# A decoder layer on one core: the context's load, the keys' tile and the routing's constants between two attentions

## The chip, the cores and the metric

The kernel runs on one core of one Trainium2 chip. The core has five engines with a queue each: TensorE (PE, matrix products; its weight loads are listed as PEld), VectorE (DVE), ScalarE (ACT), GpSimd (POOL) and SyncE (SP, which here only issues transfers). The metric is the device time of one execution in microseconds (us). An engine works through its own instructions in their order and waits where an operand is not ready; the framework puts semaphores between the engines.

## The reference

The layer takes x (16 batches of 128 tokens, 256 wide) and a context (16 batches of 128 positions, 64 wide), all float32. Cut to what matters:

```python
# 1. gated delta rule: 16 key heads, 32 value heads of 128, a scan over 128 tokens
mixed = silu(conv4(x @ w_qkv)); q, k, v = split(mixed); z = x @ w_z
S = S * exp(g);  S = S + k (v - k S) beta;  o = q S
x = layernorm(x + (rms_norm(o * silu(z)) * norm_w) @ w_out)
# 2. cross attention: 32 query heads of 8, 8 key heads; keys = values = context
x = layernorm(x + softmax(q k^T / sqrt(8)) v)
# 3. seven routed experts, each token to its best two, and one shared expert
u = x @ Wup + bup; g = silu(u @ Wgate + bgate) * u; y = g @ Wdown + bdown
x = layernorm(x + sum_e p_e * y_e + shared(x))
```

## The kernel before

The tokens of a batch lie on the 128 partitions; x stays in SBUF as `acc` (128 x 16 x 256) for the whole program.

**First attention.** Sixty-four units (four groups of four batches, times 16 key heads) go through a pipeline written as one loop over steps `s` (from L577 on). A step works on several units at once, each in another state: projections and convolution, decay products, blockwise solution of the triangular system, output. On SP the loop issues for later units the loads of weights (`wkq` L311, `wv` L324, `wz` L329, `wo` L334) and of decays (`dec` L316). GpSimd inverts the small triangular blocks (L275, L277) and takes powers for norms (L459, L106). In this loop GpSimd runs in the order in which the program is written (`manual_schedule`); the other engines' orders are planned by the framework ahead of time from its own estimates, so that instructions can be placed earlier than where they are written.

The output weights are scaled once: `scale_wo` (L160 to L171) is written in steps 5 to 12, eight rounds, each for two heads. A round loads two parts of `w_out` into the tile `wor` (one buffer, so that a round's loads wait for the stores of the round before), scales it on ScalarE (L168) and stores both parts to DRAM (`wo_d`, L170). Units load them from there.

The attention ends with a layer norm of the last four batches: statistics, a power on GpSimd (L106), and one pass per batch on VectorE (L111).

**Between the attentions.** The first attention's pools are closed and new ones opened over the same memory; in the trace nothing is written there before the attention's last accumulation (L471) has ended. Then come, as written: the context's load into `ctx_sb` (L678 to L680), the loads of the experts' weights on SP (L687 to L696), the tile `vext` with all 16 batches' keys, padded to 32 columns a head (cleared, ones in column 8, keys copied in, L707 to L711), the two query tiles `xq` cleared (L713 to L715), and the constants that only the routing needs: `zero` and its 12 transfers that clear the routed rows `xg` (L723 to L729), `tri`, `allones`, `ival`, `full` (L730 to L740), `probs`, `wrev` and `count` (L855 to L1020).

**Second attention.** Per batch, class `Cross`. `keys` spreads the context four times (`crep`, L754, GpSimd), turns it and the batch's part of `vext` on TensorE (L758, L759), copies the result on ScalarE (`kt`, L762) and masks it on GpSimd (`km`, L765). `queries` turns x1 on TensorE (L773), copies it on ScalarE (`x1T`, L775) and copies it into one of two padded tiles on GpSimd (`xq`, L777). Then, in 64 steps of two heads, `largest` computes scores and their maxima (L787, L791), `shifted` writes the maxima into `xq` and turns it (L795, L801), `exps` computes scores again and their exponentials (L810, L815), `weighted` multiplies these by `vext` (L824), and `end` and `back` bring the result into `acc` (L834 to L850). The loop that writes this runs from n = -7 on, with `largest` seven steps ahead of `exps`. In it `keys` and `queries` of batch 0 are written ahead of the loop, of batch 1 at n = -5, of batch 2 at n = -1, of batch 3 at n = 3. GpSimd's written order starts at n = 0. What is written before that, GpSimd's part of batches 0 to 2, is placed by the planner.

Routing and experts follow: scatter of rows to the experts by indirect transfers on GpSimd's queue (L1007), experts on 44 row tiles, gather, shared expert, last layer norm.

Of the kernel before, what the change touches and what calls it, by code (L numbers as in the profile page):

```python
# [8 lines left out]
F32 = mybir.dt.float32  # L9
# [3 lines left out]
ALU = mybir.AluOpType  # L13
# [3 lines left out]
P = 128  # L17
B, S, H = 16, 128, 256
HK, HV = 16, 32
G = 4  # L20
# [3 lines left out]
NE = 8  # L24
# [8 lines left out]
TILES = (2 * HB * P - (NE - 1)) // P + NE - 1  # L33
# [8 lines left out]
def decoder_kernel(  # L42
# [7 lines left out]
    nc = tc.nc  # L50
    vec, act, pool, pe = nc.vector, nc.scalar, nc.gpsimd, nc.tensor

    const = ctx.enter_context(tc.tile_pool(name="const", bufs=1))
    big = ctx.enter_context(tc.tile_pool(name="big", bufs=1))


    ident = const.tile([P, P], F32, name="ident")
# [22 lines left out]


    acc = big.tile([P, B, H], F32, name="acc")
    xv = x.rearrange("b s h -> s b h")

    def load_x(g):
        nc.sync.dma_start(out=acc[:, g * G : (g + 1) * G, :], in_=xv[:, g * G : (g + 1) * G, :])
# [28 lines left out]
    with ExitStack() as st:  # L115
# [28 lines left out]
        sb = st.enter_context(tc.tile_pool(name="sb", bufs=2))  # L144
# [14 lines left out]

        def scale_wo(i):  # L160

            wor = sb.tile([P, 2, G, P], F32, tag="wor", bufs=1, name=f"wor{i}")
            wor = wor.rearrange("p k b t -> p k (b t)").rearrange("p k (r n) -> p k r n", r=2)
            for k in range(2):
                hk = 2 * i + k
                nc.sync.dma_start(out=wor[:, k], in_=w_out[hk * 256 : (hk + 1) * 256, :]
                                  .rearrange("(r p) n -> p r n", p=P))
            act.activation(wor, wor, AF.Copy, scale=normw)  # L168
            for k in range(2):
                nc.scalar.dma_start(out=wo_d[2 * i + k], in_=wor[:, k])  # L170
# [376 lines left out]
        with tc.manual_schedule(engines={mybir.EngineType.Pool}):  # L547
            for s in range(NU + DELAY + 3):
                a, v, m = at(s), at(s - DELAY + 1), at(s - DELAY)
                p, q, o = at(s - DELAY - 1), at(s - DELAY - 2), at(s - DELAY - 3)  # L550
# [4 lines left out]
                k, ph = s // U - 1, s % U  # L555
# [32 lines left out]
                    at(s + 1).load_dec()  # L588
                if 0 < s < NG:
                    load_x(s)  # L590
                if s == U:
                    piece(0)
                    gates([1, 2, 3])
# [73 lines left out]
    late = ctx.enter_context(tc.tile_pool(name="late", bufs=1))  # L667
# [7 lines left out]
    def bank2(shape, name):  # L675
        return ps2.tile(shape, F32, tag="ps", name=name)

    ctx_sb = cx1.tile([P, B, 8, 8], F32, name="ctx_sb")  # L678
    nc.sync.dma_start(out=ctx_sb.rearrange("p b k d -> p b (k d)"),
                      in_=ctx_512.rearrange("b s d -> s b d"))  # L680

    wup = late.tile([P, NE, 2, H], F32, name="wup")
    wgt = late.tile([P, NE, 2, H], F32, name="wgt")
# [15 lines left out]
    for i, src in enumerate((bsu, bsg)):  # L699
# [4 lines left out]

    vext = cx1.tile([P, B, 8, 32], F32, name="vext")  # L707
    pool.memset(vext, 0.0)
    pool.memset(vext[:, :, :, 8:9], 1.0)
    pool.tensor_copy(vext[:, :, :, 0:8].rearrange("p b k d -> p (b k) d"),  # L710
                     ctx_sb.rearrange("p b k d -> p (b k) d"))  # L711

    xqs = [cx1.tile([P, 4, 8, 32], F32, name=f"xq{i}") for i in range(2)]  # L713
    for t in xqs:
# [5 lines left out]
    dram2 = ctx.enter_context(tc.tile_pool(name="dram2", bufs=1, space=DRAM))  # L720
    xg = [dram2.tile([TILES * P, H], F32, name=f"xg{h}") for h in range(NH)]
    yg = [dram2.tile([TILES * P, H], F32, name=f"yg{h}") for h in range(NH)]
    zero = late.tile([P, 4, H], F32, name="zero")  # L723
    pool.memset(zero, 0.0)
    for t in xg:
        for i in range(0, TILES, 4):
            n = min(4, TILES - i)
            nc.sync.dma_start(out=t[i * P : (i + n) * P, :].rearrange("(t p) d -> p t d", p=P),
                              in_=zero[:, :n, :])  # L729
    tri = late.tile([P, P], F32, name="tri")  # L730
    pool.memset(tri, 1.0)
    pool.affine_select(out=tri, in_=tri, pattern=[[1, P]], compare_op=ALU.is_ge, fill=0.0,
                       base=-1, channel_multiplier=-1)
    allones = late.tile([P, P], F32, name="allones")
    pool.memset(allones, 1.0)
    ival = late.tile([P, TILES], F32, name="ival")
    for i in range(TILES):
        pool.memset(ival[:, i : i + 1], float(i))
    full = late.tile([P, NE], F32, name="full")
    vec.tensor_scalar(full, ival[:, :NE], float(P), None, ALU.mult)  # L740

    class Cross:


# [4 lines left out]

        def keys(self):  # L750
            bi = self.bi

            crep = cx.tile([P, 8, 4, 8], F32, tag="crep", name=f"crep{bi}")
            pool.tensor_copy(crep, bc(ctx_sb[:, bi, :, None, :], [P, 8, 4, 8]))  # L754
            crf = crep.rearrange("p k g d -> p (k g d)")
            pkt = bank2([P, 2, 2, P], f"pkt{bi}")
            for c in range(2):
                pe.transpose(pkt[:, 0, c, :], crf[:, c * P : (c + 1) * P], ident)  # L758
                pe.transpose(pkt[:, 1, c, :],  # L759
                             vext[:, bi, 4 * c : 4 * c + 4, :].rearrange("p k d -> p (k d)"), ident)  # L760
            self.kt = cx.tile([P, 2, 2, P], F32, tag="kt", bufs=3, name=f"kt{bi}")
            act.copy(self.kt, pkt)  # L762
            self.km = cx.tile([P, 2, 4, P], F32, tag="km", name=f"km{bi}")
            for c in range(2):
                pool.tensor_tensor(self.km[:, c], bc(self.kt[:, 0, c, None, :], [P, 4, P]),  # L765
                                   bc(g_mask[:, :, None], [P, 4, P]), ALU.mult)
# [51 lines left out]
        def weighted(self, kvs):  # L818

            for kv in kvs:  # L820
                if kv % 4 == 0:
                    self.pav = pav_pool.tile([P, 4, P], F32, tag="pav", name=f"pav{self.bi}_{kv}")
                r = (kv % 4) * 32
                pe.matmul(self.pav[r : r + 32].rearrange("p g t -> p (g t)"),  # L824
                          lhsT=vext[:, self.bi, kv, :],
                          rhs=self.ex.pop(kv).rearrange("p g t -> p (g t)"), start=True, stop=True)
                if kv % 4 == 3:
                    self.end(kv // 4)
# [23 lines left out]

    NR = NE - 1
    probs = late.tile([P, B, NE], F32, name="probs")
    pool.memset(probs, 1.0)  # L855
    pT = late.tile([NE, B, P], F32, name="pT")
    wrev = late.tile([P, NR], F32, name="wrev")
    for e in range(NR):
        pool.memset(wrev[:, e : e + 1], float(NR - e))

    class Route:

# [153 lines left out]
        return [late.tile(shape, dt, name=f"{name}{h}") for h in range(NH)]  # L1016

    count = per_half([P, NR], "count")
    for t in count:
        pool.memset(t, 0.0)  # L1020
    ranks = per_half([P, HB, NR], "ranks")
    chosen = per_half([P, 2, HB, NR], "chosen")
    rows = per_half([P, 2, HB], "rows", U32)
# [10 lines left out]
    LEAD = 7  # L1034
    crosses = [Cross(bi) for bi in range(B)]
    steps = [(bi, (2 * h, 2 * h + 1)) for bi in range(B) for h in range(4)]
    crosses[0].keys()
    crosses[0].queries()
    later = {}
    for n in range(-LEAD, len(steps) + 3):  # L1040
        if n == 0:
            in_order = ctx.enter_context(ExitStack())
            in_order.enter_context(tc.manual_schedule(engines={mybir.EngineType.Pool}))
        if 0 <= n + 1 < len(steps) and (n + 1) % 4 == 0:
            crosses[(n + 1) // 4].shifted()
# [185 lines left out]
    r = routes[NG - 1]  # L1231
# [67 lines left out]
```

## Time and profile before

| what | us |
|---|---|
| time, median of three runs | 2191.08 (2190.01 to 2192.49) |
| the profiled execution's own time | 2189.38 |
| its span, first to last instruction | 2186.8 |
| TensorE busy | 2040.9 (93%) |
| VectorE, ScalarE, GpSimd busy | 1740.3, 1316.1, 1077.0 |
| start, 0 to 130: TensorE busy | 57.95 of 130.00 |
| first attention's body, 130 to 1743.5: TensorE busy | 1578.11 of 1613.50 |
| between, 1743.5 to 1758.8: TensorE busy | 0.05 of 15.30 |
| second attention, 1758.8 to 1959.4: TensorE busy | 193.68 of 200.60 |
| rest, experts and end, 1959.4 to 2186.8: TensorE busy | 211.13 of 227.40 |

A profile shows one execution. In its timeline a line gives start, length, engine, line of the program, operation, output and inputs with shapes, and in brackets how long the engine was idle before and which engine's instruction ended that. Stretches give, for each engine, busy time and number of instructions; then TensorE's granted clock (1.00 is full), the share of the transfer engines and GB/s. An idle stretch is put down to the signal that came last, by inference; lines of waits give total, number and longest.

### The profile page before, as it was taken

The page shows a single profiled execution, that of the slowest core. Times are in us where ns is not written, and L with a number is a line of the kernel's source. Part 1 is how long each engine was busy: PE and PEld are TensorE (multiplying, and loading weights), DVE is VectorE, ACT ScalarE, POOL GpSimd, SP SyncE. Part 2 cuts the span into 40 slices and gives each one's busy share as a digit, 9 for nine tenths or more (in the row PEclk, how much of TensorE's full clock was granted, in tenths as well). Part 3 has the DMA queues.
Part 4 walks back from the last instruction along what each step waited for, and adds up shares of the span by engine and source line. Part 5 has one row for each costly group of instructions (what it writes and reads, how often), then busy time and mean ns, then how long its engine had stood idle before and what let it go on. Part 6 is the DMA issues. An engine that isn't in the chain of part 4 may idle for free.

```text
span 2186.8 us, 40366 instructions
## 1 busy us (share of the span) xinstructions
PE 2040.9 (93%) x14688; PEld 1242.5 (57%) x14688; DVE 1740.3 (80%) x3223; ACT 1316.1 (60%) x2696; POOL 1077.0 (49%) x1639
## 2 busy tenths in 40 slices
PE   4559999999999999999999999999989879989997
PEld 2324556566565666665666656656656534448873
DVE  4657889898999989898999989898856667866545
ACT  4536666667666667666676666676656445554431
POOL 0136473838465564739384655648372143352222
PEclk7779999999999999999999999999999979999998
DMA  6412222222222222222221222222011070013321
GB/s 195 137 48 54 59 59 71 61 65 66 59 64 68 64 64 64 62 69 59 68 64 59 71 61 68 64 59 59 30 40 30 23 262 1 1 56 105 110 80 58
DMA packets 140660, 150.72 MB, mean 69 GB/s; under 512 B 14184, under 2 KB 111472, under 8 KB 140464
## 3 DMA queue, kind: packets, MB, share of 16 engines
q1 hardware_dynamic: 133456, 135.37, 21.9%
q0 software_dynamic: 3072, 8.39, 1.2%
q10 hardware_dynamic: 3936, 4.38, 0.6%
q8 instruction: 118, 1.93, 0.4%
q14 instruction: 78, 0.64, 0.1%
HBM read 125.82 MB, written 22.28 MB: 68 GB/s over the span
## 4 chain that ended last, share of the span: by engine, by line
PE 72%; POOL 10%; DVE 8%; ACT 4%; issue 3%; DMA 3%; SPq 0%; ACTq 0%; POOLq 0%; DVEq 0%
PE pp L467 9%; PE pjv L339 8%; PE pjz L339 8%; PE pjkq L339 8%; PE pt L520 6%; PE po L452 5%; PE pu L505 5%; PE pk L399 4%; PE psc L787 3%; POOL Tp L277 2%; POOL tmp L275 2%; PE pv L439 2%; PE psq L482 2%; PE prg L1123 2%; PE pru L1123 2%
## 5 line engine op out<-in xcount | busy, mean ns | idle before, releaser
L524 ACT COPY u<-pt 32x512 f32<-32x512 f32 x512 | 294.4, 575 | 57.1 <-PE pt L520 48.4
L339 PE MATMUL pjkq<-xT,wkq 128*128 128x512 f32 x512 | 246.0, 621 | 55.9 <-issue 47.3
L509 DVE TENSOR_TENSOR u<-u,pu 32x512 f32<-32x512 f32 x384 | 263.6, 687 | 37.9 <-PE pu L505 27.0
L365 POOL TENSOR_TENSOR yv<-yv,y2v 128x508 f32<-128x508 f32 x128 | 161.8, 1264 | 255.2 <-DVE yv L356 231.8
L467 PE MATMUL pp<-wo,og 128*128 128x256 f32 x1024 | 272.1, 395 | 0.0
L277 POOL TENSOR_TENSOR Tp<-Tp,tmp 128x240 f32<-128x240 f32 (+14 forms) x465 | 253.6, 545 | 36.4
L275 POOL TENSOR_TENSOR tmp<-Tp 128x240 f32<-128x240 f32 (+14 forms) x465 | 239.6, 515 | 62.0 <-DVE Tp L277 33.8
L356 DVE SCALAR_TENSOR_TENSOR ykq<-pjkq,cw,ykq 128x504 f32<-128x504 f32 (+2 forms) x384 | 266.2, 725 | 2.8 <-ACT ykq L349 2.3
L356 DVE SCALAR_TENSOR_TENSOR yv<-pjv,cw,yv 128x504 f32<-128x504 f32 (+1 forms) x256 | 188.9, 738 | 98.7 <-ACT y2v L353 91.6
L339 PE MATMUL pjv<-xT,wv 128*128 128x512 f32 x512 | 250.2, 612 | 16.8 <-issue 7.0
L471 DVE SCALAR_TENSOR_TENSOR acc<-pp,rstd,acc 128x256 f32<-128x256 f32 x512 | 231.5, 477 | 42.9 <-POOL rstd L459 37.1
L459 POOL TENSOR_TENSOR rstd<-var,m_half 128x8 f32<-128x8 f32 x64 | 105.4, 1648 | 320.7 <-DVE ss L493 272.3
L339 PE MATMUL pjz<-xT,wz 128*128 128x512 f32 x512 | 243.7, 598 | 5.9 <-issue 5.9
L366 ACT ACTIVATE vT<-yv 128x512 f32<-128x512 f32 x128 | 80.7, 630 | 252.2 <-POOL yv L365 252.2
L467 PEld LDWEIGHTS pp<-wo,og 128*128 128x128 f32 x1024 | 183.5, 190 | 78.5 <-issue 57.2
L339 PEld LDWEIGHTS pjkq<-xT,wkq 128*128 128x128 f32 x512 | 93.1, 194 | 184.1 <-issue 173.9
L402 DVE TENSOR_TENSOR lp<-pk,e 128x512 f32<-128x512 f32 x256 | 159.3, 682 | 39.7 <-PE pk L399 38.6
L520 PE MATMUL pt<-u,Tt 32*32 32x128 f32 x4096 | 176.2, 272 | 1.6 <-ACT u L442 1.0
L520 PEld LDWEIGHTS pt<-u,Tt 32*32 32x32 f32 x4096 | 116.4, 104 | 105.5 <-issue 35.1
L384 DVE TENSOR_TENSOR_SCAN e<-dec,ident 128x512 f32<-128x512 f32 x128 | 158.4, 1278 | 8.2 <-DMA dec<-dec_d 6.5
L452 PE MATMUL po<-lp,u 128*128 128x128 f32 x1024 | 152.2, 285 | 0.0
L442 ACT ACTIVATE u<-pv,nk 128x128 f32<-128x128 f32 x512 | 147.3, 374 | 6.5 <-PE pv L439 5.8
(226 smaller groups left out, 3619.6 us busy)
## 6 DMA issues: line engine op xcount, KB each, us to landing
dec<-dec_d SPq DMA_DIRECT2D x64, 512.0 KB, 5.2
wkq<-in_L_attn_w_qkv_dram SPq DMA_DIRECT2D x128, 128.0 KB, 5.1
wv<-in_L_attn_w_qkv_dram SPq DMA_DIRECT2D x64, 256.0 KB, 2.6
wz<-in_L_attn_w_z_dram SPq DMA_DIRECT2D x64, 256.0 KB, 2.6
wo<-wo_d SPq DMA_DIRECT2D x64, 256.0 KB, 2.7
rx<-xg SPq DMA_DIRECT2D x44, 128.0 KB, 2.1
yg<-ry SPq DMA_DIRECT2D x44, 128.0 KB, 1.7
xg<-zero SPq DMA_DIRECT2D x10, 512.0 KB, 7.8
```

The costliest lines, as they stand in the source:

```text
L275: eng.tensor_tensor(tv, bc(T[:, j + 1 :, j : j + 1], [P, n, j]), bc(T[:, j : j + 1, 0:j], [P, n, j]), ALU.mult)
L277: return eng.tensor_tensor(T[:, j + 1 :, 0:j], T[:, j + 1 :, 0:j], tv, ALU.add)
L339: pe.matmul(pj.rearrange("p b t -> p (b t)"), lhsT=ws[kc], rhs=xTs[self.g][:, kc, :], start=(kc == 0), stop=(kc == 1))
L356: inst = vec.scalar_tensor_tensor(out=y[:, :, d:], in0=pj[:, :, : P - d], scalar=c[:, k : k + 1], in1=y[:, :, d:], op0=ALU.mult, op1=ALU.add)
L365: pool.tensor_tensor(y[:, :, 1:], y[:, :, 1:], y2[:, :, 1:], ALU.add)
L402: self.made = vec.tensor_tensor(self.lp[:, r, hf * 2 : hf * 2 + 2], pk, bc(self.e[r][:, hf * 2 : hf * 2 + 2, None, :], [P, 2, 2, P]), ALU. ...
L452: pe.matmul(po[:, b, :], lhsT=self.u_[r][:, b, :], rhs=self.lp[:, r, b, 1, :], start=True, stop=True)
L467: pe.matmul(pp[:, r, :], lhsT=self.og[:, r, b, :], rhs=self.wo[:, r, :], start=True, stop=True)
L471: vec.scalar_tensor_tensor(out=a, in0=pp[:, r, :], scalar=self.rstd[:, r, b : b + 1], in1=a, op0=ALU.mult, op1=ALU.add)
L509: vec.tensor_tensor(u.u_[r][blk], u.u_[r][blk], pu[blk], ALU.subtract)
L520: pe.matmul(pt[blk, b, :], lhsT=groups[u.n // U].Tt[blk, 8 * u.u + G * r + b, :], rhs=u.u_[r][blk, b, :], start=True, stop=True)
L524: act.copy(u.u_[r][blk], pt[blk])
```

## The change

Four things change. (1) `ctx_sb` is made at the top, in the pool that lives through the program; the eight rounds of `scale_wo` use it as their tile `wor`, and the context is loaded into it in step 48 of the first attention's loop. (2) `vext` becomes four tiles of one batch each; all four are cleared and given their ones before the second attention, and `keys` copies its batch's keys into one of them in turn. (3) The routing's constants are written at n = 1 of the second attention's loop, behind `keys` and `queries` of batch 2. (4) GpSimd's written order starts ahead of `keys` of batch 0.

```diff
     acc = big.tile([P, B, H], F32, name="acc")
+    ctx_sb = big.tile([P, B, 8, 8], F32, name="ctx_sb")
...
         def scale_wo(i):
-            wor = sb.tile([P, 2, G, P], F32, tag="wor", bufs=1, name=f"wor{i}")
-            wor = wor.rearrange("p k b t -> p k (b t)").rearrange("p k (r n) -> p k r n", r=2)
+            wor = ctx_sb.rearrange("p b k d -> p (b k d)").rearrange("p (k r n) -> p k r n", k=2, r=2)
...
                 if 0 < s < NG:
                     load_x(s)
+                if s == 3 * HK:
+                    nc.sync.dma_start(out=ctx_sb.rearrange("p b k d -> p b (k d)"),
+                                      in_=ctx_512.rearrange("b s d -> s b d"))
...
-    ctx_sb = cx1.tile([P, B, 8, 8], F32, name="ctx_sb")
-    nc.sync.dma_start(out=ctx_sb.rearrange("p b k d -> p b (k d)"),
-                      in_=ctx_512.rearrange("b s d -> s b d"))
...
-    vext = cx1.tile([P, B, 8, 32], F32, name="vext")
-    pool.memset(vext, 0.0)
-    pool.memset(vext[:, :, :, 8:9], 1.0)
-    pool.tensor_copy(vext[:, :, :, 0:8].rearrange("p b k d -> p (b k) d"),
-                     ctx_sb.rearrange("p b k d -> p (b k) d"))
+    vexts = [cx1.tile([P, 8, 32], F32, name=f"vext{i}") for i in range(4)]
+    for t in vexts:
+        pool.memset(t, 0.0)
+        pool.memset(t[:, :, 8:9], 1.0)
...
         def keys(self):
             bi = self.bi
+            self.vext = vexts[bi % 4]
+            pool.tensor_copy(self.vext[:, :, 0:8], ctx_sb[:, bi])
...
+    in_order = ctx.enter_context(ExitStack())
+    in_order.enter_context(tc.manual_schedule(engines={mybir.EngineType.Pool}))
     crosses[0].keys()
     crosses[0].queries()
     later = {}
     for n in range(-LEAD, len(steps) + 3):
-        if n == 0:
-            in_order = ctx.enter_context(ExitStack())
-            in_order.enter_context(tc.manual_schedule(engines={mybir.EngineType.Pool}))
+        if n == 1:
+            pool.memset(probs, 1.0)
+            for e in range(NR):
+                pool.memset(wrev[:, e : e + 1], float(NR - e))
+            for t in count:
+                pool.memset(t, 0.0)
+            zero = late.tile([P, 4, H], F32, name="zero")
+            pool.memset(zero, 0.0)
+            for t in xg:
+                for i in range(0, TILES, 4):
+                    k = min(4, TILES - i)
+                    nc.sync.dma_start(out=t[i * P : (i + k) * P, :].rearrange("(t p) d -> p t d", p=P),
+                                      in_=zero[:, :k, :])
+            tri = late.tile([P, P], F32, name="tri")
+            pool.memset(tri, 1.0)
+            pool.affine_select(out=tri, in_=tri, pattern=[[1, P]], compare_op=ALU.is_ge, fill=0.0,
+                               base=-1, channel_multiplier=-1)
+            allones = late.tile([P, P], F32, name="allones")
+            pool.memset(allones, 1.0)
+            ival = late.tile([P, TILES], F32, name="ival")
+            for i in range(TILES):
+                pool.memset(ival[:, i : i + 1], float(i))
+            full = late.tile([P, NE], F32, name="full")
+            vec.tensor_scalar(full, ival[:, :NE], float(P), None, ALU.mult)
```

The same constants' lines are removed from where they stood, and the products with the keys' tile (L824) and its transposes (L759) read the batch's own tile.

More of the change, by code (lines that the diff above doesn't have):

```diff
@@ L722, in decoder_kernel @@
     yg = [dram2.tile([TILES * P, H], F32, name=f"yg{h}") for h in range(NH)]
[L723 to L740, printed above, removed]
     class Cross:
@@ L759, in keys @@
                 pe.transpose(pkt[:, 1, c, :],
-                             vext[:, bi, 4 * c : 4 * c + 4, :].rearrange("p k d -> p (k d)"), ident)
+                             self.vext[:, 4 * c : 4 * c + 4, :].rearrange("p k d -> p (k d)"), ident)
             self.kt = cx.tile([P, 2, 2, P], F32, tag="kt", bufs=3, name=f"kt{bi}")
@@ L824, in weighted @@
                 pe.matmul(self.pav[r : r + 32].rearrange("p g t -> p (g t)"),
-                          lhsT=vext[:, self.bi, kv, :],
+                          lhsT=self.vext[:, kv, :],
                           rhs=self.ex.pop(kv).rearrange("p g t -> p (g t)"), start=True, stop=True)
@@ L854, in decoder_kernel @@
     probs = late.tile([P, B, NE], F32, name="probs")
-    pool.memset(probs, 1.0)
     pT = late.tile([NE, B, P], F32, name="pT")
     wrev = late.tile([P, NR], F32, name="wrev")
-    for e in range(NR):
-        pool.memset(wrev[:, e : e + 1], float(NR - e))
     class Route:
@@ L1018, in decoder_kernel @@
     count = per_half([P, NR], "count")
-    for t in count:
-        pool.memset(t, 0.0)
     ranks = per_half([P, HB, NR], "ranks")
```

## The prediction

> **What bounds the kernel now.** I read the page's 40 slices first. Each is 54.7 us. The first line is TensorE's busy tenths, the second its granted clock:
>
> ```profile
> PE   4559999999999999999999999999989879989997
> PEclk7779999999999999999999999999999979999998
> ```
>
> From the fourth slice on TensorE is 8 or 9 tenths busy at nearly full clock, apart from slice 33 (1749 to 1804 us), where both digits are 7, and the last. So a change beside TensorE pays only at the start and at that dip. The dip lies between the two attentions. The waits of 1743 to 1790 us name it (total, times, longest):
>
> ```profile
> PE pkt L758 <- POOL crep L754: 15.3, 1, 15.3
> ```
>
> TensorE's last matmul of the first attention ends at 1743.55 and its next is at 1758.80: 15.25 us for a copy by GpSimd. GpSimd's timeline shows what stood before that copy (start, length):
>
> ```profile
> 1742.49 1.64 POOL L459 TENSOR_TENSOR rstd<-var,m_half 128x8 f32<-128x8 f32 x1 [7.25 <-DVE var L490]
> 1747.67 3.51 POOL L708 MEMSET vext<- 128x4096 f32 x1 [3.54 <-DVE acc L471]
> 1751.28 1.01 POOL L106 TENSOR_TENSOR rsa<-rsa,m_half 128x4 f32<-128x4 f32 x1
> 1752.24 0.95 POOL L715 MEMSET xq<- 128x1024 f32 x1
> 1753.12 0.31 POOL L709 MEMSET vext<- 128x128 f32 x1
> 1753.30 0.99 POOL L715 MEMSET xq<- 128x1024 f32 x1
> 1754.24 1.08 POOL L710 COPY vext<-ctx_sb 128x1024 f32<-128x1024 f32 x1
> 1755.27 1.09 POOL L724 MEMSET zero<- 128x1024 f32 x1
> ...
> 1758.35 0.40 POOL L754 COPY crep<-ctx_sb 128x256 f32<-128x256 f32 x1
> ```
>
> The reader is to see no idle time from 1747.67 on: GpSimd is the bound, not the context's transfer, which was issued at 1747.48 and landed 4.9 us later, at 1752.4, when GpSimd still had 5.9 us to do. (The chain of waits puts weights' transfers here. ScalarE's first copy of keys, which it hangs on them, reads only TensorE's transposes, over 0.03 us before.) VectorE runs beside, twice held:
>
> ```profile
> 1749.16 2.04 DVE L105 TENSOR_SCALAR rsa<-mva 128x4 f32<-128x4 f32 x1
> 1752.32 4.50 DVE L111 TENSOR_SCALAR acc<-acc,mva,rsa 128x256 f32<-128x256 f32 x4 [1.12 <-POOL rsa L106]
> ```
>
> The medians of these two lines are 0.17 and 0.40 us. The first ended at 1751.20, when the memset of 3.51 us ended (1751.18). Last, the clock in stretches (length, TensorE, its loads, VectorE, ScalarE, GpSimd, then clock, DMA share, GB/s):
>
> ```profile
> 1743.55:1747.39 3.84, 0.00 (x0) 0.00 (x0) 3.23 (x9) 0.00 (x0) 0.57 (x1) 1.00 0.00 0
> 1747.39:1758.80 11.41, 0.00 (x0) 0.00 (x1) 9.18 (x14) 0.00 (x0) 11.03 (x44) 0.56 0.75 193
> 1758.80:1772.60 13.80, 12.43 (x46) 6.38 (x46) 7.23 (x13) 2.30 (x5) 5.84 (x9) 0.50 1.10 353
> 1772.60:1782.20 9.60, 9.04 (x60) 4.19 (x59) 6.30 (x11) 6.95 (x12) 2.43 (x3) 1.00 1.05 393
> ```
>
> Half clock outlasts the gap by 13.8 us of dense work.
>
> **The change, part by part.** *Keys' tile and constants.* Ahead of the first crep go away: 3.51 + 0.31 + 1.08 us of the big vext, and the constants, 1755.27 to 1758.35 = 3.08. Together 7.98. Added are four memsets of 256 columns. 4096 columns take 3.51 and 1024 take 0.97, so 0.83 ns a column and 0.125 us fixed: 0.34 each, 1.36. Four memsets of ones, 128x8, by wrev's row (seven in 0.30): 0.17. One copy of 64 columns; 1024 take 1.08 and crep's 256 take 0.40, so 0.22. Together 1.75. Net 7.98 - 1.75 = 6.23 us: crep would end at 1752.5 instead of 1758.75.
>
> What is late next? rsa's power (1.01) stands in the same line, and its input is ready at about 1749.4 if VectorE is not held; the four keys' tiles are cleared by 1749.2. It waits 0.2 us, or a memset of xq slips ahead of it: I take off 0.2, leaving **6.0**. The four layer-norm passes must end before the queries' transposes. From 1751.4 (power after one xq memset) they need 4 x 0.40, plus 0.97 if held by the other: 1754.0. The first score needs the keys' side: transposes 1.1, ScalarE's copy 0.6, the first mask 1.05, with hand-overs 2.97 us in this trace (1758.75 to 1761.72), so 1755.5 in the new order; the queries' side ends at about 1754.0 + 0.6 + 0.4 = 1755.0. Keys still decide, by 0.5.
>
> *Context loaded earlier.* Of the gap it removes nothing by itself: the 4.9 us were covered by GpSimd. It makes room, because the new crep (begun at 1752.1) would otherwise wait for 1752.4. The moved step is one DMA on SP's queue: 0.38 us of issue, 512 KB, ahead of the loads of wv, wz, wo and the next dec. Between 1014 and 1077 us SP issues six loads in a step of 25 us, and no scan there waited for dec; cost 0, and 4.9 if that cover were gone. It needs the scaled output weights, now in the same tile, to be stored; the last store is issued by about 101 us. On the weights' loads it was moved past: wup can start 0.4 us sooner; nothing uses them before the expert stage.
>
> *wor in ctx_sb.* Same eight rounds of load, scale, store. This part may matter more than it looks: early on, the chain of waits runs through it, and SP's row says how long its queue stood:
>
> ```profile
> SPq L166 <- DMA wo_d<-wor: 41.5, 8, 9.9
> ```
>
> With halves of one tile, the first half's load can wait for the first half's store alone. At best one issue (0.45) goes from each of the four rounds between 42 and 78 us: 1.8 us. At worst another order of SP's queue adds one such wait, 9.9. I take 0, since each scale needs both halves as before.
>
> *GpSimd in written order.* Now km of batch 0 (waiting for ScalarE) stands before crep of batches 1 and 2, and both before the constants. In times counted from the end of crep 0, with the trace's own waits: km0 ends at 3.9, crep 1 at 4.9 (its transposes came at 6.7); km1 ends at 10.5, crep 2 at 11.5 (14.9); km2 18.3, xq2 18.7, constants 21.8, vext and crep of batch 3 by 22.4 (transposes 23.4). Slack 1.0 us: cost 0, with up to 3.1 if the constants are not covered. Queued behind the constants are crep 3 and km3; TensorE's scores of batch 3 wait for them. From there on one copy of 0.22 a batch is added, 16 x 0.22 = 3.5 us, beside GpSimd's idle stretches of 4.8 us in each 10 us batch; the turn of four is free too: batch 0's last product with vext ends by 1785.8, crep 4 at 1789.1. The zeros' 12 DMAs leave later than 1770.6 but are due only at the scatter after 1900.
>
> *A rule against it.* The shared GpSimd and VectorE rows above say: held for the rest of one GpSimd instruction. [...]
>
> **Sum.** The profiled execution took 2189.38 (span 2186.8 + 2.6 around). 2189.4 - 6.0 = 2183.4. The median of the three runs, 2191.08, stands 1.7 above it: 2185.1 there.
>
> **Rivals.**
> 1. *Slower: SP's early queue.* wor's new home lets the planner put another load between the halves, or the context's load with its wait for the last stores ahead of one that is due. Price 9.9 (longest such wait) - 6.0 = +3.9: 2195. For: the early chain is made of these waits. Against: rounds and data are the same, and behind the last store GpSimd's inversion runs to 123 us as cover. It decides from 6 us on.
> 2. *Half a gain.* If the clock returns at a fixed moment (1772.6), not after an amount of work, 6 us more are run at half clock and yield 3: 2188. The same figure comes if the constants' 3.1 us stall batch 3. For: half clock lasted through 9 us of dense TensorE work. Against: the granted clock fell after idling, so it follows the work.
> 3. *Another wait takes its place.* The memsets still first, layer norm held by every GpSimd piece (4.50 again): passes end at 1755.9, first score 1757.2, gain 4.5, and 2.4 if crep 3 is then late by the constants' 3.1 less the slack of 1.0: 2188.7.
> 4. *More.* crep ahead of both xq memsets (1.9 more) and the 1.8 early: 2181.4.
>
> **Numbers.** Forecast 50 in 100, own range 2182.5 to 2187. Rivals 1 to 4: 15, 16, 9, 10. A measurement of this kernel tells 0.2% (4.4 us) from no change; faster means below 2186.7. Faster: forecast and rival 4, 60; same: 2 and 3, 25; slower: 15. The 8-in-10 range reaches to rival 4's end with the runs' own spread (2180.5) and up to 2193, half-way from no change (2191.1) to rival 1 (2195).
>
> **What would show it.** TensorE's gap after 1743.5 near 9.3 us; crep within 5.2 us of GpSimd's first memset; L105 near 0.2 us; the constants after xq2 with crep 3 not waited for; half clock still some 14 us. I am wrong if the early chain up to 123 us moves by over 2 us, if TensorE waits for crep or km of batches 1 to 3, or if the gap shrinks and the end doesn't follow.

## The result, and the profile after

The changed kernel takes 2195.16 us (median, 2191.29 to 2198.65), the kernel before in the same runs 2190.15. The ratio is 1.002, 95% interval 1.0014 to 1.0026: slower by 0.2%, some 5 us, where 6 us less were forecast. The profiled execution took 2197.14 (span 2194.5).

The dip between the attentions did become shorter. The same two rows of the 40 slices (TensorE's busy tenths, its granted clock; each slice is now 54.9 us):

```profile
PE   4559999999999999999999999999989989989997
PEclk8668999999999999999999999999999989999998
```

Slice 33 is one tenth busier than before (8 for 7) and has clock 8 for 7; but at the start the clock's first four digits are 8668 for 7779. The waits of that stretch (total, times, longest), where the kernel before had 15.3 in the first line:

```profile
PE pkt L741 <- POOL crep L737: 8.7, 1, 8.7
...
DVE full L1044 <- POOL ival L1042: 2.6, 1, 2.6
PE psc L770 <- POOL km L748: 1.9, 2, 1.4
PE pst L793 <- DVE mx L774: 1.8, 1, 1.8
```

The first line is the forecast gain: 15.25 - 8.66 = 6.6 us. The second and fourth are new, and one follows from the other. GpSimd's timeline of the stretch (start, length):

```profile
1756.90 0.56 POOL L710 MEMSET vext<- 128x256 f32 x2 [3.54 <-DVE acc L472]
...
1758.94 0.95 POOL L715 MEMSET xq<- 128x1024 f32 x1
1759.85 1.00 POOL L107 TENSOR_TENSOR rsa<-rsa,m_half 128x4 f32<-128x4 f32 x1
1760.82 0.23 POOL L734 COPY vext<-ctx_sb 128x64 f32<-128x64 f32 x1
1760.99 0.40 POOL L737 COPY crep<-ctx_sb 128x256 f32<-128x256 f32 x1
...
1779.50 0.40 POOL L760 COPY xq<-acc 128x256 f32<-128x256 f32 x1
...
1781.83 0.80 POOL L1042 MEMSET ival<- 128x1 f32 x22
```

From the first memset to the end of `crep` are now 1761.39 - 1756.90 = 4.49 us, before 11.08. But everything stands later: the first memset at 1756.90 for 1747.67, **9.2 us behind the kernel before**. Half of the question is therefore what happened ahead of 1743 us, in a part where the forecast put nothing.

Followed back along GpSimd, 9.2 to 9.3 us are there from the second of its powers (`rstd`) on and stay so to the end of the attention; 7.7 at the first power, and 6.6 at GpSimd's first inversion, which starts at 106.13 for 99.55. The 2.6 us between lie in a stretch in which the granted clock was lower (0.85 for 0.93 from 130 to 250 us). Ahead of the inversion, ScalarE and TensorE of the kernel before (50 to 72 us):

```profile
56.15 1.34 ACT L361 ACTIVATE kq<-ykq 128x512 f32<-128x512 f32 x2 [4.61 <-DVE ykq L356]
59.89 1.15 ACT L168 ACTIVATE wor<-wor,normw 128x1024 f32<-128x1024 f32 x1 [2.40 <-DMA wor<-in_L_attn_w_out_dram]
...
58.05 2.39 PE L399 MATMUL pk<-kq 128*128 128x256 f32 x8
```

and of the changed kernel, with SP's queue:

```profile
55.00 0.63 ACT L362 ACTIVATE kq<-ykq 128x512 f32<-128x512 f32 x1 [4.70 <-DVE ykq L357]
59.34 1.15 ACT L169 ACTIVATE ctx_sb<-ctx_sb,normw 128x1024 f32<-128x1024 f32 x1 [3.71 <-DMA ctx_sb<-in_L_attn_w_out_dram]
60.39 0.61 ACT L362 ACTIVATE kq<-ykq 128x512 f32<-128x512 f32 x1
...
61.06 3.78 PE L400 MATMUL pk<-kq 128*128 128x256 f32 x8 [3.94 <-ACT kq L362]
```

```profile
53.12 0.37 SPq L167 DMA_DIRECT2D ctx_sb<-in_L_attn_w_out_dram  x1
53.59 0.41 SPq L317 DMA_DIRECT2D dec<-dec_d  x1
54.05 11.64 SPq L167 DMA_DIRECT2D ctx_sb<-in_L_attn_w_out_dram  x3
68.00 0.88 SPq L312 DMA_DIRECT2D wkq<-in_L_attn_w_qkv_dram  x2
```

The reader is to see three things. In SP's queue a load of `dec` now stands between the two halves of a round of output weights (round 3 of the eight, counted from 0); before, a round's two loads stood together. On ScalarE the scaling of that round stands between the two activations `kq`, which were one group before, and waits 3.71 us for the load. TensorE's products `pk` wait 3.94 us for the second `kq`; before, they started 3 us sooner and without that wait. The scaling itself is the same instruction of 1.15 us and starts no later than before (59.34 for 59.89); late is only what stands behind it in the list.

This first delay does not last: TensorE's transposes `pxT` begin at 76.17 us for 74.84, 1.3 us late. At round 5 ScalarE's list has a second change. Before, the copy into `xT`, which TensorE needs, stood ahead of the scaling:

```profile
75.94 0.58 ACT L136 COPY xT<-pxT 128x512 f32<-128x512 f32 x1 [4.06 <-PE pxT L133]
77.49 1.15 ACT L168 ACTIVATE wor<-wor,normw 128x1024 f32<-128x1024 f32 x1 [0.97 <-DMA wor<-in_L_attn_w_out_dram]
```

and in the changed kernel it stands behind it:

```profile
78.95 1.15 ACT L169 ACTIVATE ctx_sb<-ctx_sb,normw 128x1024 f32<-128x1024 f32 x1 [5.02 <-DMA ctx_sb<-in_L_attn_w_out_dram]
80.50 0.58 ACT L137 COPY xT<-pxT 128x512 f32<-128x512 f32 x1 [0.40 <-ACT ctx_sb L169]
81.14 0.43 PE L191 MATMUL pab<-wba,xT 128*128 128x64 f32 x2 [2.52 <-ACT xT L137]
```

The scaling comes 1.5 us later, the copy behind it 4.6, and `gtu`, which is made from these products, 5.4 (94.84 for 89.49). In this trace most of the 6.6 us at the inversion comes in here.

Where the time goes then, as offsets of the changed kernel's profile against the one before: GpSimd's first inversion +6.6, first memset between the attentions +9.2, mask of batch 0 +2.6, of batch 2 +2.5, of batch 3 +6.5, end +7.7.

### The profile page after: what moved, and what is told of

It reads as the page before. It is cut to its first block, busy times and chain, and to the rows that moved or that the text cites. A ratio compares the mean times of both kernels' runs of the same rounds, so it can differ in the third digit from the quotient of the medians.

```text
span 2194.5 us, 40381 instructions
## 1 busy us (share of the span) xinstructions
PE 2052.8 (94%) x14688; PEld 1247.9 (57%) x14688; DVE 1734.8 (79%) x3223; ACT 1316.8 (60%) x2696; POOL 1075.5 (49%) x1660
## 4 chain that ended last, share of the span: by engine, by line
PE 72%; POOL 10%; DVE 8%; ACT 4%; issue 3%; DMA 3%; SPq 0%; ACTq 0%; POOLq 0%; DVEq 0%
PE pp L468 9%; PE pjv L340 8%; PE pjz L340 8%; PE pjkq L340 8%; PE pt L521 6%; PE po L453 5%; PE pu L506 5%; PE pk L400 4%; POOL Tp L278 2%; POOL tmp L276 2%; PE psc L770 2%; PE pv L440 2%; PE psq L483 2%; PE prg L1125 2%; PE prd L1125 2%
## 5 line engine op out<-in xcount | busy, mean ns | idle before, releaser
L362 ACT ACTIVATE kq<-ykq 128x512 f32<-128x512 f32 x128 | 80.6, 630 | 121.0 <-DVE ykq L357 110.5
```

## The experiments

Two theories were set against the trace. A: the tile shared by context and output weights makes the waits of the eight rounds finer (a half waits for its own half's store), and the planner then lays SP's and ScalarE's lists out otherwise; that costs what stands ahead of 1743 us. B: VectorE's product `full`, which reads the last constant, now stands in VectorE's list behind GpSimd's constants and ahead of maxima that TensorE needs. The rival to A was that the early transfer of the context costs the time (C).

The first eight runs are on two chips on which the kernel before takes 2190.72 and 2191.36 us.

**1. The shared tile alone**, with the context's early load that belongs to it, in the kernel before:

```diff
+    ctx_sb = big.tile([P, B, 8, 8], F32, name="ctx_sb")
-            wor = sb.tile([P, 2, G, P], F32, tag="wor", bufs=1, name=f"wor{i}")
...
+            wor = ctx_sb.rearrange("p b k d -> p (b k d)").rearrange("p (k r n) -> p k r n", k=2, r=2)
...
+                if s == 3 * HK:
+                    nc.sync.dma_start(out=ctx_sb.rearrange("p b k d -> p b (k d)"),
...
```

> Before, with part 1 alone (wor in ctx_sb, context loaded in step 48). Theory A (the halves of the shared tile are waited for one by one, so the planner puts SP's and ScalarE's early instructions in another order): the first attention ends 9.2 us later than in the kernel before, as in the changed kernel; the gap of TensorE stays 15.2 us, since GpSimd bounds it; time +9 (about 2199). Rival R (the early delay is the chance timing of one execution, or comes from parts 2 to 4 through the planner): attention's end unchanged, time 2190.

Measured 2198.51 against 2190.72, ratio 1.0039 (1.0026 to 1.0052): **+7.8 us from this part alone**, the gap unchanged (15.3). In its profile the attention ends only 4.5 us late (first memset 1752.20 for 1747.67), not the 9.2 expected; the mask of batch 3 is 7.1 us late, behind a stretch at half clock of 34.1 us where before has 23.9, ten steps for seven (last section). The picture ahead of the inversion is that of the changed kernel:

```profile
60.09 1.15 ACT L168 ACTIVATE ctx_sb<-ctx_sb,normw 128x1024 f32<-128x1024 f32 x1 [4.43 <-DMA ctx_sb<-in_L_attn_w_out_dram]
61.14 0.61 ACT L361 ACTIVATE kq<-ykq 128x512 f32<-128x512 f32 x1
...
61.81 3.41 PE L399 MATMUL pk<-kq 128*128 128x256 f32 x8 [4.67 <-ACT kq L361]
```

**2. All but the shared tile**: the changed kernel with `wor` in its own tile again and the context loaded behind the attention.

```diff
-            wor = ctx_sb.rearrange("p b k d -> p (b k d)").rearrange("p (k r n) -> p k r n", k=2, r=2)
+            wor = sb.tile([P, 2, G, P], F32, tag="wor", bufs=1, name=f"wor{i}")
...
+    ctx_sb = cx1.tile([P, B, 8, 8], F32, name="ctx_sb")
+    nc.sync.dma_start(out=ctx_sb.rearrange("p b k d -> p b (k d)"),
...
```

> The changed kernel with part 1 undone (wor a tile of its own, context loaded after the attention). Theory A: first attention ends where it ended before (last pp products end near 1743.6 in the profile); gap of TensorE 8.7 us, or up to 9.4 where the keys' copy waits for the context's landing 5.0 us after the attention's last accumulation; then 3.9 us lost again at the wait of VectorE for ival, and 1 later: time -1 to -2, about 2189. Rival R: attention later by 9 us here too, time 2195.

2189.44 against 2190.72, ratio 0.9995 (0.9985 to 1.0004). SP's early list is that of the kernel before. The gap is 9.8 us, 1.1 more than in the changed kernel, 0.8 of it the copy into `vext` waiting for the context, which without the early load lands late. The gain is lost again further on: the mask of batch 0 is 2.8 us earlier than before, that of batch 3 1.0 us later, with TensorE waiting 1.2 us for a maximum, so B is at work here too.

**3. The waits as before, tile shared**: the first load of a round is made to wait for both stores of the round before it.

```diff
+                for st_ in stores[-2:] if k == 0 else ():
+                    tc.add_manual_dep(load.ins, st_.ins.name, ...)
...
+                stores.append(nc.scalar.dma_start(out=wo_d[2 * i + k], in_=wor[:, k]))
```

> The changed kernel, with the first load of each round of scale_wo made to wait for both stores of the round before, as the separate tile did; all else as changed, the context's early load too. Theory A: early delay gone, inversion on GpSimd begins near 99.6 us instead of 106.1, the whole 9.2 us come back: about 2186. Rival C (the context's own transfer in SP's early queue is what delays): still late by 6 or more, 2193 to 2195.

2187.77, ratio 0.9986 (0.9977 to 0.9995). One more wait in each round makes the kernel **0.34% faster than the changed one, 7.4 us of 2190**. The context is still loaded early (102.84 us in this trace), so C falls. ScalarE's two `kq` stand together again, and TensorE does not wait for them:

```profile
55.65 1.33 ACT L367 ACTIVATE kq<-ykq 128x512 f32<-128x512 f32 x2 [4.44 <-DVE ykq L362]
59.31 1.15 ACT L174 ACTIVATE ctx_sb<-ctx_sb,normw 128x1024 f32<-128x1024 f32 x1 [2.33 <-DMA ctx_sb<-in_L_attn_w_out_dram]
...
57.55 2.99 PE L405 MATMUL pk<-kq 128*128 128x256 f32 x8
```

The masks of batches 0 to 2 are 6.1 us earlier than before, that of batch 3 only 2.1: here, with A out of the way, B's 4.1 us stand alone.

**4. `full` on GpSimd**, in the changed kernel:

```diff
-            vec.tensor_scalar(full, ival[:, :NE], float(P), None, ALU.mult)
+            pool.tensor_scalar(full, ival[:, :NE], float(P), None, ALU.mult)
```

> The changed kernel with full (8 columns) computed on GpSimd behind ival instead of on VectorE. Theory B (VectorE's line stands 2.6 us behind full, which waits for constants that GpSimd now makes after xq of batch 2, and TensorE's scores behind VectorE's maxima): mask of batch 3 comes 2.6 us later than before instead of 6.5, time -3.9 against the changed kernel, about 2191. Rival (another limit stands there, for instance the written order of GpSimd): under 1 us comes back.

2192.52, ratio 1.0008 (0.9999 to 1.0017): 0.12% less than the changed kernel, 2.6 us. GpSimd does the product in 0.24 us. TensorE's wait for `mx` is gone from its waits, and the masks of batches 2 and 3 stand at +1.3 and +1.25: nothing is lost between them. B holds. Its size is less sure: 2.6 us here (the intervals of the two kernels overlap), 0.16% or 3.5 us from run 3 to run 5, 0.24% or 5.2 us from run 2 to run 6, and the profiles show 4.

**5. Both cures**, runs 3 and 4 together:

> The changed kernel with both cures: the first load of a round waits for both stores of the round before, and GpSimd, not VectorE, multiplies ival into full. If the two causes are the whole of the loss and independent, the 3.9 us that the run with the first cure alone gives back at the scores of batch 3 stay: batch 3's mask is 6 us earlier than in the kernel before, and the median is 2187.8 - 2.6 to 3.9 = 2184 to 2185.2, ratio 0.997 to 0.9975 against before. Rival: what TensorE is spared between the attentions is taken back further on by another wait; then the median stays at 2187 to 2188 with batch 3's mask 6 us early all the same.

2184.46 against 2191.36, ratio **0.997 (0.9958 to 0.9982)**: 6.9 us faster than the kernel before. The masks of batches 0 and 3 are 4.8 and 5.2 us earlier than before, and TensorE's waits between 1735 and 1810 us hold the gap and the mask, but no wait for a maximum:

```profile
PE pkt L746 <- POOL crep L742: 8.7, 1, 8.7
...
PE psc L775 <- POOL km L753: 1.9, 2, 1.4
```

The two causes add up: 0.20% of the changed kernel, less 0.34% and 0.12%, gives -0.26%; measured is -0.30%.

**6. The other way to both cures**: run 2 with `full` on GpSimd (the edits of runs 2 and 4).

> The changed kernel without the shared tile (the scaled weights' rounds have their own tile, the context is loaded after the attention), and full on GpSimd. Both causes are gone here as well, but GpSimd's copy into vext waits for the context's transfer for some 0.8 us. Expected: median 2189.4 - 2.6 = 2186.8 down to 2185.5 (a full 3.9 less), about 1 to 2 us above the run with the waits put back, and the gap of TensorE near 9.8 us. Rival: the early load of the context costs something elsewhere; then this run is level with that one or faster.

2186.17, ratio 0.9971 (0.9959 to 0.9982), gap 9.6. Level with run 5 within the intervals, as far as these tell: the early load of the context is worth at most the 1 us that the gap shows.

**7. The shared tile, the load of the context written behind the attention:**

```diff
-                if s == 3 * HK:
-                    nc.sync.dma_start(out=ctx_sb.rearrange("p b k d -> p b (k d)"),
...
+    nc.sync.dma_start(out=ctx_sb.rearrange("p b k d -> p b (k d)"),
+                      in_=ctx_512.rearrange("b s d -> s b d"))
```

> The changed kernel, tile shared, but the context loaded only behind the attention as before. If the halves' finer waits alone upset SP's order, the first inversion of GpSimd starts 4 to 7 us late and the median is 2195 to 2197, not below the changed kernel's (the transfer adds the 0.8 us wait of vext's copy). If the early transfer, by its bytes or its place in SP's queue, has a share in the loss, the median falls below 2194.

2196.17, ratio 1.0023 (1.0014 to 1.0032). A miss as a test of C: the planner issued the load at 105.28 us all the same (105.76 in the changed kernel), since nothing but the last stores of the output weights holds it back.

So runs 3 and 5 decide on C, not this one. What it shows is that the place in the source of that load decides nothing once the tile lives through the program.

**8. The written order from step 0 on**, as before, with both cures:

```diff
-    in_order = ctx.enter_context(ExitStack())
-    in_order.enter_context(tc.manual_schedule(engines={mybir.EngineType.Pool}))
     crosses[0].keys()
...
+        if n == 0:
+            in_order = ctx.enter_context(ExitStack())
+            in_order.enter_context(tc.manual_schedule(engines={mybir.EngineType.Pool}))
```

> Both cures, and the written order of GpSimd begun at step 0 as in the kernel before. In GpSimd's list batch 0's mask now stands behind the clearing of probs, count and zero (about 3 us) and behind the copies of context of batches 1 to 3. If the written order is worth what the list shows, TensorE waits for batch 0's mask by 2 to 4 us and the median is 2 to 4 us above the run with both cures (2186 to 2189). Rival, the prediction's own figure: the order is covered and costs nothing; then the two are level within 1 us.

2187.60, ratio 0.9984 (0.9975 to 0.9993): 3.1 us above run 5. The planner puts the clearing of `zero` and the copies for the next batches ahead of the first mask, and TensorE waits for it:

```profile
1755.83 0.94 POOL L1034 MEMSET zero<- 128x1024 f32 x1
1756.72 0.39 POOL L742 COPY crep<-ctx_sb 128x256 f32<-128x256 f32 x1
1757.08 2.03 POOL L753 TENSOR_TENSOR km<-kt,g_mask 128x512 f32<-128x512 f32 x2
```

```profile
PE psc L775 <- POOL km L753: 2.8, 1, 2.8
```

The prediction's "cost 0" for the written order is right, but close to half of run 5's gain hangs on it (3.1 of 6.9 us).

**9 to 11. Which displaced load does it.** The wait of run 3 for some of the rounds only. These three and run 12 fell to another chip, on which the kernel before takes 2214.93 us (run 9 spends 23 us more than run 3 between 1995 and 2086 us, among the experts, with waits of TensorE that run 3 does not have, and runs 10 to 12 show such waits too; why is not known), so only ratios are compared.

```diff
+                for st_ in stores[-2:] if k == 0 and i >= 3 else ():
```

> The changed kernel with the wait for both stores put back for rounds 3 to 7 only. SP's list then differs from the one with all waits back in one place: a load of wo still stands between the halves of round 1. If the harm is done by the later displaced loads, this run is level with the run with all waits back, 2187.8 within 1 us. If the split of round 1 (22 to 26 us) carries it, the median is 2193 to 2196 as in the changed kernel.

2211.12, ratio 0.9979 (0.9969 to 0.9989): as with all waits back, in the ratio. The load of `wo` that still stands inside round 1 does no harm.

```diff
+                for st_ in stores[-2:] if k == 0 and i >= 6 else ():
```

> The wait for both stores put back for rounds 6 and 7 only. SP's list keeps all of the changed kernel's displaced loads up to round 5: wo between the halves of round 1, a load of dec between the halves of round 3, and round 5 and both halves of the next ones ahead of the weights wkq 6, whose load the changed kernel issues 6.2 us later than the kernel before (89.03 for 82.80). If wkq 6 behind those loads carries the loss, the median is 2193 to 2196. Rival: the loss comes from the last rounds and the context's load behind them; then it falls to 2187 to 2189.

2216.17, ratio 1.0003 (0.9993 to 1.0012): between the two theories' figures, and by itself inconclusive.

```diff
+                for st_ in stores[-2:] if k == 0 and i >= 5 else ():
```

> The wait for both stores put back for rounds 5 to 7. Against the run before this in the list, wkq 6 comes again ahead of the last two rounds; what stays is wo inside round 1 and dec inside round 3, with wkq 5 some 2.8 us late (68.00 for 65.22). If wkq 6 carries the loss alone, 2187 to 2189; if wkq 5's 2.8 us count in full, 2190 to 2191; if neither, 2193 to 2196.

2219.04, ratio 1.0019 (1.0010 to 1.0027): as slow as the changed kernel, though the weights `wkq` 6 stand again ahead of the last two rounds in SP's list. That theory falls: `wkq` 6 is issued late (88.84 us) because the work before it is late. SP's lists of this run and run 9 differ in one place, `dec` between the halves of round 3, and ScalarE's list follows it in two places: there, and at round 5, whose scaling stands ahead of the copy into `xT` in run 11 (80.94, then 82.00) and behind it in run 9 (75.85, then 77.98). The first of them, run 9, ScalarE:

```profile
54.29 1.34 ACT L367 ACTIVATE kq<-ykq 128x512 f32<-128x512 f32 x2 [4.18 <-DVE ykq L362]
59.36 1.15 ACT L174 ACTIVATE ctx_sb<-ctx_sb,normw 128x1024 f32<-128x1024 f32 x1 [3.73 <-DMA ctx_sb<-in_L_attn_w_out_dram]
```

then run 11, ScalarE and TensorE:

```profile
54.73 0.63 ACT L367 ACTIVATE kq<-ykq 128x512 f32<-128x512 f32 x1 [3.87 <-DVE ykq L362]
60.37 1.15 ACT L174 ACTIVATE ctx_sb<-ctx_sb,normw 128x1024 f32<-128x1024 f32 x1 [5.01 <-DMA ctx_sb<-in_L_attn_w_out_dram]
61.43 0.61 ACT L367 ACTIVATE kq<-ykq 128x512 f32<-128x512 f32 x1
...
62.09 3.78 PE L405 MATMUL pk<-kq 128*128 128x256 f32 x8 [5.25 <-ACT kq L367]
```

In run 9 TensorE starts `pk` at 56.20, in run 11 at 62.09: 5.9 us, and GpSimd's first inversion follows 5.5 us later (105.53 for 99.98). In between the delay shrinks to 3.0 us (the scaling of round 5, 80.94 for 77.98) and is 4.7 again at `gtu` (94.65 for 89.93). One changed place in SP's list, with what the planner made of it in ScalarE's, is the loss. Which of the two swaps on ScalarE costs how much is not shown: all six traces of the slower order (the changed kernel, runs 1, 4, 7, 10 and 11) have both, the eight others have neither. Why run 10, which has this swap too and starts its inversion at 106.22, is 0.16% faster than run 11 in the medians, stays open.

**12. `crep` ahead of the clearing of `xq`**, with both cures:

```diff
+            for t in xqs if bi == 0 else ():
+                pool.memset(t, 0.0)
...
```

(in `keys`, behind the copy into `crep`; the two memsets before it go)

> Both cures, and the two clearings of xq (1.9 us) written behind crep of batch 0 in GpSimd's list. TensorE's gap shrinks from 8.7 to 6.5 to 7 us. If the queries' side (power, four layer-norm passes, transposes, copy) now decides, the first score comes only 0 to 0.7 us sooner and the median is 2183.5 to 2184.5. If the keys' side still decides, as in the prediction's rival of more gain, all 1.9 us arrive: 2182.6 or, with one window of 3.41 us less at half clock, 2181.

2204.92 against 2214.93, ratio **0.9955 (0.9942 to 0.9969)**, the fastest of all in the ratio, though its interval overlaps that of run 5. TensorE's gap falls from 8.7 to 5.9 us, but a wait for the mask takes part of it back (3.1 us for 1.4), so the first score comes 6.4 us after the first memset for 7.5 in run 5: 1.1 of the 1.9 us arrive. (In the medians run 12 is 0.15% or 3.3 us below run 5, but the profiled execution here, 2211.09, is the slowest of its six: the size is open.)

The queries' side is not what holds the rest: its transposes `px` begin at 1754.92. ScalarE holds it. It issues small loads of weights and biases from its own queue, and its copy of the keys begins 0.04 us behind the last of them, though the transposes that it reads had ended at 1755.13:

```profile
1755.06 0.60 ACTq L708 DMA_DIRECT2D bd<-in_L_ffn_bdown_dram  x1
...
1756.42 0.24 ACTq L709 DMA_DIRECT2D bd<-in_L_ffn_bsd_dram  x1
1756.71 0.59 ACT L750 COPY kt<-pkt 128x512 f32<-128x512 f32 x1 [11.24 <-DMA wup<-in_L_ffn_Wup_dram]
```

In run 5 the last issue had ended at 1754.00 and the copy began 0.04 us behind the transposes (1755.17). The last line puts the wait down to the landing of `wup`, by inference; the order and the times speak for the issues, but no run moves them, so this is argued and not shown. GpSimd, which clears `xq` until 1756.91, could have begun the mask (1757.37) 0.46 us sooner at best. VectorE's instructions take longer as well, beside GpSimd's work:

```profile
1753.76 1.16 DVE L106 TENSOR_SCALAR rsa<-mva 128x4 f32<-128x4 f32 x1
1756.05 2.70 DVE L112 TENSOR_SCALAR acc<-acc,mva,rsa 128x256 f32<-128x256 f32 x4 [1.13 <-POOL rsa L107]
```

The four passes take 2.70 us here and 1.61 in run 5. The first takes 1.01, beside the clearing of `xq` (1755.96 to 1756.91), and the last 1.12, beside the mask (1757.37 to 1758.59); the two between take 0.39 to 0.40 each.

## Why the prediction was wrong

**Keys' tile and constants, -6.0: right.** The gap of TensorE fell by 6.6 us (9.3 was forecast for it, 8.66 came), `crep` ended 4.5 us after the first memset (within 5.2), the power stood behind both memsets of `xq` rather than one, which cost nothing, and the passes were hardly held (1.60 for 4.50). VectorE's L105, now L106, took 0.59 and not 0.2: it ended at 1758.99, with GpSimd's clearing of `xq` (1758.01 to 1758.96). One premise was wrong and did no harm: "The four layer-norm passes must end before the queries' transposes". The passes are of the last four batches, the first queries of batch 0; in the changed kernel the transposes begin at 1762.35 and the passes end at 1762.50, and in run 12 the transposes begin before the passes. So the queries' side of the sum, and rival 3's with it, rested on a wait that is not there. With the two causes below removed, the whole kernel gains 0.30% (0.18 to 0.42), 6.6 us (3.9 to 9.2): the forecast's 6.0 lies well within.

**wor in ctx_sb, "I take 0, since each scale needs both halves as before": the step that failed.** Alone it costs 7.8 us, by its interval 5.7 to 11.4; the step's own bounds were -1.8 and +9.9. The sentence is true of the data and says nothing of the order. The lists of SP and ScalarE are planned from estimates of when things are ready, and a half that can be loaded earlier is given an earlier place in SP's queue, the next free slot goes to `dec`, and the scaling, planned for an earlier moment, is put ahead of an activation, and two rounds later of a copy, that TensorE waits for. On the chip the load is later than planned (in the changed kernel ScalarE waits 3.71 us for it in round 3 and 5.02 in round 5), and everything behind it in ScalarE's list waits along. The waits are measured; the planner's reasons are argued from its lists. Rival 1 named this way and the sign, at 15 in 100. That its figure, 2195, came out is luck, since the terms are others: its 9.9 less 6.0 was +3.9; the runs say +7.8 for the order, +2.6 to 5.2 for `full`, about -6.6 for the rest: +3.8 to +6.4, around the 5.0 of the medians. Its argument against itself, the inversion to 123 us as cover, fails because the delay arises in rounds 3 and 5, ahead of the inversion.

**GpSimd in written order, cost 0: right as far as it went, but not costed whole.** Counted from the end of the first `crep`, the masks of batches 0 to 2 kept their times, and TensorE did not wait for `crep` or the mask of batch 3. What was left out is an instruction of another engine that belongs to the moved block: `full` on VectorE. Its row of before stood in the trace (0.90 us at 1757.54, waiting for `ival`), in a stretch in which VectorE had nothing else. Moved behind the keys and queries of batch 2 it waits 2.59 us in VectorE's list with maxima behind it; the line of before, then those of the changed kernel:

```profile
1757.54 0.90 DVE L740 TENSOR_SCALAR full<-ival 128x8 f32<-128x8 f32 x1 [0.71 <-POOL ival L738]
...
1782.20 0.45 DVE L1044 TENSOR_SCALAR full<-ival 128x8 f32<-128x8 f32 x1 [2.59 <-POOL ival L1042]
1782.28 2.48 DVE L774 TENSOR_REDUCE mx<-psc 128x4 f32<-128x512 f32 x4
```

TensorE waits 1.80 us for these maxima, and then the clock falls too, to 0.50 from 1785.07 to 1788.48 (below). Rival 3 had a wait by the constants' 3.1 less 1.0 us of slack, 2.1, but at `crep` of batch 3; the size is near, the engine was another.

**Context loaded earlier, cost 0: right, in another place.** It was issued at 105.8 us and not between 1014 and 1077; run 6 against run 5 gives it nothing that can be told.

**A rule against it: it cost nothing here.** The moved memset of `zero` ran from 1780.28 to 1781.23, when the small product into `xq` had ended (1779.61). VectorE's instructions did take longer beside GpSimd's work in other places: L106 here 0.59 us for a median of 0.17, to the end of the clearing of `xq`, and in run 12 the first pass beside a clearing and the last beside a mask, by 0.6 and 0.7 us. In the kernel before, the first of the four passes took 2.11 us from 1752.32 on, beside three memsets (to 1754.29), so "the rest of one GpSimd instruction" is too short for it. What a memset beside the product into `xq` would do no run shows.

**Half clock, still some 14 us: right.** 13.40 us from the first transpose on, before 13.80. In run 5 it was 12.9 us and in run 8 23.1, so that it came so close is in part luck.

Of the conditions named for being wrong, the first came true: the early chain moved by over 2 us.

## What to carry to other kernels

When a tile is given a new home, ask what the dependencies become, not only whether the data still fit: finer waits can let a planner re-order queues far from the change, and a load that is planned too early on one engine holds what stands behind it in another engine's list (ScalarE waited 3.71 and 5.02 us here); putting the coarser wait back took 7.4 us off the changed kernel here. When a block is moved on one engine, list every reader of what it makes on the other engines as well, and see what is queued behind each of them. And a gain in one stage and a loss in another are told apart by offsets of the same instruction in two traces, before any theory.

## What was not expected of the hardware

**The clock changed in steps of 3.41 us.** The stretch at half clock around the gap was 17.1 us long in the changed kernel and in runs 5, 9, 10 and 11, 23.9 in the kernel before and in runs 6 and 12, 27.3 in run 8 and 34.1 in run 1: 5, 7, 8 and 10 times 3.41. In the changed kernel's trace the steps keep their grid: the clock falls at 23.80 and at 1757.76, 508 steps apart. A step in which TensorE was only partly busy was enough there. Stretches of the changed kernel behind the wait for `full`, one grid step each (length; TensorE, its loads, VectorE, ScalarE, GpSimd; clock, share of the transfer engines, GB/s):

```profile
1778.24:1781.65 3.41, 2.61 (x14) 1.32 (x14) 1.34 (x3) 3.17 (x6) 3.33 (x16) 1.00 1.08 396
1781.65:1785.07 3.42, 2.05 (x11) 0.46 (x11) 2.56 (x5) 0.80 (x2) 1.49 (x26) 1.00 1.00 393
1785.07:1788.48 3.41, 3.41 (x20) 2.08 (x16) 0.69 (x1) 1.17 (x2) 0.00 (x0) 0.50 1.09 385
```

TensorE was busy 2.05 of 3.42 us in the second, and the third runs at half clock. Busy time alone does not decide: in the kernel before, the step from 1741.82, with TensorE busy 1.73 of 3.41 us, is followed by one with 0.00 that is still at full clock. So a stall of 1.8 us can cost up to 1.7 more, by an estimate from these rows (3.41 us at clock 0.50, half a step), and 1.8 became about 4 in the profile. From the mask of batch 2 to that of batch 3 it is 9.0 us in the kernel before and in run 4; 13.1 in the changed kernel and in runs 9, 10 and 11, where the clock falls to 0.50 in between for one step, and in run 3; 11.5 in runs 2 and 7.

How many busy steps went by before the full clock came back differs: in run 1 five with TensorE busy for their whole 3.41 us were at half clock (1767.97 to 1785.03), in the kernel before three (1762.29 to 1772.53), in run 5 two (1760.08 to 1766.91) behind one with 3.15.

```profile
1750.90:1785.04 34.14, 20.32 (x72) 10.38 (x75) 21.05 (x37) 6.67 (x12) 19.31 (x55) 0.50 0.92 305
```

This line is run 1's stretch of ten steps; what decides between two and five is open. Single profiles differ by some us, perhaps by such steps, which is not shown: the start of the first inversion lay between 98.3 and 103.2 us in the traces with the order of before, and between 103.3 and 106.2 in those with the swapped one, so sizes are taken from the medians and places from the traces.
